# One transformer layer on sixteen images: the order of all five engines taken from written lists

## The chip, the cores and the metric

The kernel runs on one core of a Trainium2 chip. The metric is the device time of one execution in microseconds; lower is better. A core has five instruction streams that run side by side and meet only at semaphores: PE (TensorE, matrix products), ACT (ScalarE, table functions such as sine and exponential), DVE (VectorE), POOL (GpSimd) and SP (SyncE, which here only issues DMA transfers). Each stream is executed strictly in the order in which the program was written, so an instruction that waits holds up everything behind it on its engine.

## What is computed

Sixteen images are cut into patches, 1024 tokens of 256 numbers each; then comes one attention layer with a special treatment of the keys, and one mixture-of-experts network. Cut to what matters here:

```python
h = patches @ W.T + b                        # 1024 tokens x 256, per image
n = layernorm(h)
q, k, v = split(n @ w_qkv)                   # 8 heads of 32
k = sum(a[f]*sin(f*k) + b[f]*cos(f*k) for f in 1..256)
attn = softmax(q @ k.T * 32**-0.5)           # 1024 x 1024 per head
h = h + (attn @ v) @ w_out + b_out
n = layernorm(h)
shared = mlp3(n)                             # 256 -> 256 -> 128 -> 256
gated = two best of four experts, weighted   # 256 -> 128 -> 64 -> 256 each
h = h + shared + gated
```

## The kernel before

The sum over 256 frequencies is not taken term by term. The angles of one key channel are written to DRAM, read back and copied over the partitions (`load_waves`, the DMA `w<-ud`), multiplied by whole numbers on POOL (`turn_waves`, L1009) and put through a sine on ACT (`sine`, L1019). PE mixes two such tiles with the coefficients into a tile `kan` of PSUM (`mix`, L1039), DVE multiplies that by a third sine tile (`times_fast`, L1053, the tile named `f`), and PE adds up the products (`add_up`, L1072). This is one group of 8 key channels; an image has 32 groups, and after every eighth the finished keys of two heads are split in a high and a low part on DVE (`finish_keys`, L617 and L618), written to DRAM (`kd`), and read back stacked (`stack_keys`, `k<-kd`).

Attention runs in rounds. A round treats two heads and 512 queries, and has eight score tiles, one for each 128 keys; an image has eight rounds. For a score tile PE makes two matmuls of 512 columns (`score`, L1137, the tile `sT`). ACT takes the exponential (`exponential`, L1154): for an even tile into SBUF (`es`), for an odd one in place in PSUM. DVE then adds the odd tile to the even one before it (`pair_sum`, L1169, the tile `both`): these are the sums of two tiles of keys, by which the denominators are added up for two key tiles at once. PE weighs the values (`weigh`, L1184: `es` with the values, `both` with the values and with ones), and DVE normalizes at the end of the round (L1208, L1213, L1225).

Two resources tie this together. The PSUM pool `big` has two buffers of 1024 columns, and both the `kan` tiles of `mix` and the score tiles take them in turn. A score tile can therefore begin only when the reader of the tile two places before it is done: the exponential for an even score tile, the pair sum for an odd one, the product L1053 for a `kan` tile. And the wave tiles have eight buffers (`NW`), so a load waits for the mix of four groups earlier.

The rest (tokens, norms, keys, queries, values, gates, networks, projection) runs as four chains of small steps, numbered 0 to 3, which use two smaller PSUM buffers. A step of a chain that may take either form (`ANY`) is made as whole 128 x 128 matmuls or as four matmuls of 32 columns side by side, whichever fits its neighbours on PE (`tiling_of`). PE works in three tilings: whole, 128 x 32 (weighing, adding up, split steps) and 64 x 32 (mixing).

All instructions are written in an order which a planner in the kernel finds before it is built. PE's order is written out by hand in `ORDER`: M is a mix, R an adding up, S a score tile, W a weighing, a digit a step of that chain; one stretch of 240 letters covers an image and is repeated eleven times. The other four engines have no list: `others` goes through SP, POOL, ACT and DVE and takes, up to PE's clock, the step that would be ready first by the planner's own clocks, with a cost for each step given by hand (`put(ACT, "fixed", 0.99, ...)`). On ACT the sines, the loading of the exponential's table (`table`) and the exponentials of a round stand in one queue, `fixed`, in the order in which they were put there; only chain steps come between them.

Of the kernel before, what the change touches and what calls it, by code (L numbers as in the profile page):

```python
# [12 lines left out]
AF = mybir.ActivationFunctionType  # L13
# [44 lines left out]
LAG, LANDS, TABLE, PER_COLUMN = 0.06, 2.0, 1.28, 1.0 / 600  # L58
SWITCH = {None: 0.21, (128, 32): 0.13, (64, 32): 0.13}

TILINGS = {"mix": (64, 32), "av": (128, 32), "red": (128, 32)}
USERS = {"M": "prod", "S": "exp"}
KINDS = {"M": "mix", "R": "red", "S": "score", "W": "av"}
COLUMNS = (128, 32)
ORDER = (
    "333333313133100003300M00M00R00MM0MR3M33",
    "RM3M33MR03MR303MMSS0WSSWRWSSS3S03WWMMWW",
    "RMWMSSSRSSSWWSSWWW3WMM0RM0WWSSSSSSSWWWSMWWWRM0WMMWMRSSSSWWSSSRWSWWWWMMWMRMSSWSSSSWSSWRW0"
    "MWMMWMWWSSSRSSWWSWRSWSWWWW0M00M0SSSWRMWSWS3SW3SMSWRW3WMWM3MRMSS1SSWSSWRSSWW3W3MMWWWMR1SS"
    "S0SSWWS3S1MSWR1WM30MWWWSWM1R01SM1WS1WWSS1RSS1S0W1W1WWWMM0RMSSS1SSW1SWSW1SMW1RWMWW01MMWM1"  # L70
    "SS1RSRSWWS1SS0S1W1MMWMMWRSWWWS1S1S0SS1WWS1S3RWW1WMW1M1WMMWSS1SRSS1RS1SWWW1SW31WWMMW3WM0S"
    "SR0S1S0SWWSS1SMW3RM1W0WMMW1RWMWSS1S3SS1SSWWRS31WWWWWWM103MS1SSW1WSRS3MSWWSSMW1WWRWM13MM1"
    "S3SSRMSWWS3WSS3R1SW0WWM1WM1W1RM0SS1SW1SSWSSWWSMW1W1RM0M1WW1MS1S1MRWS1SWRSWS0SS1WM1WMWWWS"
    "S0RM3S1WMS1SWWSS0SWRW3WW10MMW31MS1SS1WRSSW1MS1SSWWWRW1WW01",
    (
        "MM0R1MM1S1SS1SSWW1S0S1SRWW0WWWWMM1MMRS3SS1SS1SSWWRSWWWWW3W13MM0RMM3SSS1SSWRWWS1SSWW3WMW3"
        "WM311MRSM1SWSSS1WR3SS31SWW0WW1WM1MW1MM0SS1SRW1SWS0S1WSSWRWWWWM01MM10RM0SS1SW1SSWW1SSWRS1"
        "WWWWMM1MS0SSWRWMSW1S1SS3SWWRW3WW1MM31MMRS1SS1WWSS1SS1SWWRWWWW101"
    )
    * 11,  # L80
    "MM10RMS3SS1SS01SSWWWSM1RWWWW1WMM01MS1MR",
    "WSS1SS3WWSS3WRSWW1WW30MM1RMS1SS3SS1SWWSSWMW3RMM311WMWMWWSRSSR3S1SSWWWS13S0WW1WWMMW1M01MS"
    "1S1SSRRSW1SW1SSWW101WMWWMWMMRSSS1SSW1WS1RWSSWWW1MM1WMSWSSR0SSWW1MS1SW1W1S10RW1MMWWW0MRMS"
    "1SS1SS1SSWW1SWR0WW1W1WMMMW1SRSS1SSWW1MSWSWS1WR1MMWWWRMS1S0SWMS1SSWSRSW0WWWWW10M1M1SS0RSS"
    "MWWSSS1SMWWR1MWW1MW1WR1MMS1SWS1SWSWSS1SRWWW1WWMMR1M1MSS1SW1SS1SWSSWRWW1M1WW1MMMWSSSRSSWS"
    "SRWWS1WWWMMRWW1MM1SS1W1S1SWSSS1SRWW1WWMWM1WM1MRS1RSWS1SWSS1SSWWWW1WW1SS1WS1SS1SSWWWSSWWW"
    "W1SS1S1SWSWSSWWWWWW11110110111110101001000000101001000100",
)

@with_exitstack  # L90
def plain_path(ctx: ExitStack, tc: tile.TileContext, a: dict, out: bass.AP, verdict: bass.AP):
# [179 lines left out]
    def retile(tiling):  # L271

        same = now["tiling"] == tiling
        now["tiling"] = tiling
        return 0.0 if same else SWITCH[tiling]

# [53 lines left out]
    def step(c):  # L330
# [9 lines left out]
        if on:  # L340
            at = max(clock[on], ch["ready"] + LAG)
            if on == PE:
                at = max(at, banks(c)[0][0] + LAG)
            ch["ready"] = clock[on] = at + (need[1] or 0.0)
            if bank is not None:
                free[bank] = ch["ready"]
        elif isinstance(need, tuple):
            ch["ready"] = max(ch["ready"], done[need])
# [11 lines left out]
        if on == PE:  # L360
            took = PER_COLUMN * (now["stream"] - before) + retile(now["piece"])
            now["piece"] = None
            ch["ready"] = clock[PE] = at + took
# [16 lines left out]
    def wanting(engine):  # L380

        for c, ch in enumerate(chains):
            need = ch["need"]
            if ch["gen"] is None or callable(need) or need[0] != engine:
                continue
            if engine == ACT and len(need) > 2 and now["table"] != need[2]:
                continue
            at = max(clock[engine], ch["ready"] + LAG)
            if engine == PE:
                if not banks(c):  # L390
                    continue
                at = max(at, banks(c)[0][0] + LAG)
            yield at, c

    def lay(engine, queue):
        cost, deps, key, action = queues[engine][queue].pop(0)
        at = begin(engine, deps)
        clock[engine] = at + cost
        done[key] = clock[engine]
        action()  # L400

    def heads(engine):
        for rank, (name, steps) in enumerate(queues[engine].items()):
            at = begin(engine, steps[0][1]) if steps else None
            if at is not None:
                yield at, rank, name

    def others(limit):

        soonest = None  # L410
        again = True
        while again:
            again = False
            soonest = None
            for engine in (SP, POOL, ACT, DVE):
                while True:
                    settle()
                    best = min(heads(engine), default=None)
                    chain = min(wanting(engine), default=None)
                    if chain and (  # L420
                        best is None
                        or chain[0] < best[0]
                        or (chain[0] == best[0] and best[2] not in ("sum", "prod", "keys"))
                    ):
                        at, lay_it = chain[0], lambda c=chain[1]: step(c)
                    elif best:
                        at, lay_it = best[0], lambda q=best[2]: lay(engine, q)
                    else:
                        break
                    if at > limit:  # L430
                        soonest = at if soonest is None else min(at, soonest)
                        break
                    lay_it()
                    again = True
        return soonest

    def lay_fixed(kind):

        cost, deps, key, action = queues[PE][kind][0]
        user = USERS.get(kind)  # L440
        if kind == "S" and key[2] % 2:
            user = "sum"
        at = begin(PE, deps + (bigs[-2:-1] if user else []))

        def lay_it():
            queues[PE][kind].pop(0)
            clock[PE] = done[key] = at + cost + retile(TILINGS.get(KINDS[kind]))
            if user:
                bigs.append((user, *key[1:]))
            action()  # L450

        return at, lay_it

    def run():

        order = "".join(ORDER)
        for i, token in enumerate(order):
            now["ahead"] = order[i + 1 : i + 4]
            while True:
                soonest = others(clock[PE])  # L460
                if token in KINDS:
                    at, lay_it = lay_fixed(token)
                else:
                    c = int(token)
                    at = next((at for at, one in wanting(PE) if one == c), None)
                    lay_it = lambda: step(c)
                if at is not None and (soonest is None or at <= max(soonest, clock[PE])):
                    break
                assert soonest is not None
                others(soonest)  # L470
            lay_it()
        while (soonest := others(clock[PE])) is not None:
            others(soonest)
        assert not any(q for e in queues.values() for q in e.values())
        assert not any(ch["gen"] for ch in chains)
# [4 lines left out]
    def load_x(b, j):  # L480

        b, j = b + j // (N // XT), j % (N // XT)
        if b < B:
# [5 lines left out]
            done["x", b, j] = transfer(1.75, 0.6, clock[PE])  # L489
# [38 lines left out]
    def tokens(b, half):  # L528
# [5 lines left out]
        for t in range(4):  # L534
# [14 lines left out]
            yield DVE, 0.41  # L549
# [95 lines left out]
    def values(b):  # L645
# [5 lines left out]
        for t0 in range(0, NT, 2):  # L651
# [12 lines left out]
            yield ACT, 0.5  # L664
# [7 lines left out]
            yield DVE, 0.6  # L672
# [134 lines left out]
    def networks(b, half, late=False):  # L807
# [25 lines left out]
        def first_of_expert(e):  # L833
            yield ANY
            ps = hidden(lambda c: w1e[:, 2 * e + c, :], "e1p")
            yield ACT, 0.6
# [4 lines left out]
        def second_of_experts(u, e1):  # L841
# [11 lines left out]
            yield ACT, 0.6  # L853
# [15 lines left out]
        for m in range(2):  # L869
            yield ANY  # L870
            ps = hidden(lambda c, m=m: w1s[:, c, ts(m, P)], "s1p")
            yield ACT, 0.6
# [14 lines left out]
        yield ACT, 0.6  # L887
# [57 lines left out]
    def load_waves(g, j):  # L945
# [13 lines left out]
        put(SP, "waves", 1.1, deps, ("load", g, j), action)  # L959
# [29 lines left out]
    def spread_waves(g):  # L989
# [11 lines left out]
        put(DVE, "spread", 1.28, deps, ("spread", g), action)  # L1001

    def turn_waves(g, j):
# [8 lines left out]
        put(POOL, "turn", 1.87, [dep], ("turn", g, j), action)  # L1012

    def sine(g, j, change):
        def action():
            now["table"] = AF.Sin
# [6 lines left out]
        put(ACT, "fixed", 0.96 + change, [("turn", g, j)], ("sine", g, j), action)  # L1023
# [26 lines left out]
    def times_fast(g):  # L1050
# [4 lines left out]
        put(DVE, "prod", 1.16, [("mix", g), ("sine", g, 2)], ("prod", g), action)  # L1055
# [76 lines left out]
    def score(att, kc):  # L1132
# [13 lines left out]
        put(PE, "S", 0.47, deps, ("score", att, kc), action)  # L1146

    def exponential(att, kc):
        def action():
            now["table"] = AF.Exp  # L1150
# [6 lines left out]
        put(ACT, "fixed", 0.99, deps, ("exp", att, kc), action)  # L1157
# [8 lines left out]
    def pair_sum(att, kc):  # L1166
# [5 lines left out]
        put(DVE, "sum", 1.16, deps, ("sum", att, kc), action)  # L1172
# [28 lines left out]
    def normalize(att):  # L1201
# [8 lines left out]
        def divide(half):  # L1210
# [11 lines left out]
            put(DVE, "norm", 0.4, deps, ("divide", att, half), action)  # L1222
# [15 lines left out]
        put(DVE, "norm", 1.67, [("av", att, NT - 1)], ("reciprocal", att), reciprocal)  # L1238
# [819 lines left out]
```

## Time and profile before

| | us |
|---|---|
| time, median of 4 runs (lowest to highest) | 3971.72 (3963.89 to 3976.18) |
| the profiled execution's own time | 3968.66 |
| its span in the profile | 3967.1 |

| engine | busy us | share of the span |
|---|---|---|
| PE, matmuls | 3728.9 | 94% |
| ACT | 3259.5 | 82% |
| POOL | 3192.2 | 80% |
| DVE | 3115.3 | 79% |
| the 16 DMA engines, hardware queue of SP | | 79.2% |

From the first mix of one image to the first mix of the next it takes, in the repeated part, 236 to 239 us. A matmul's end in the profile is modelled, and matmuls overlap; the time at which PE begins one is the surer number. "PEld" is the loading of a matmul's weights, which runs beside the matmul before it.

### The profile page before, as it was taken

What the parts mean: (1) busy time and instruction counts of PE and PEld (TensorE: products, weight loads), DVE (VectorE), ACT (ScalarE), POOL (GpSimd) and SP (SyncE); (2) the same over time, 40 slices, a digit from 0 to 9 for tenths busy, and PEclk for the clock granted to TensorE, in tenths of its full rate; (3) what the DMA queues carried; (4) which work ended last, traced back from release to release, by engine and by line L of the source; (5) the groups of instructions that cost most, each with busy time, mean ns of one, the idle gap of its engine ahead of it and who ended that gap; (6) DMA issues with size and microseconds to landing.
All of it is one profiled execution on the core that took longest, in us unless ns stands there. A gap on an engine that the chain in (4) does not pass through costs nothing. (4 is left out here: it accounts for less than half of the span.)

```text
span 3967.1 us, 93620 instructions
## 1 busy us (share of the span) xinstructions
PE 3728.9 (94%) x35701; PEld 1810.2 (46%) x35701; DVE 3115.3 (79%) x4715; ACT 3259.5 (82%) x3875; POOL 3192.2 (80%) x2312
## 2 busy tenths in 40 slices
PE   7888999999999999999999999999999999999988
PEld 4324344454544545444454544545454454534434
DVE  4667878888787887878878787888878888787873
ACT  2687888888888888898888888888888888888983
POOL 4878888788887888878888888878878888888860
PEclk9899999999999999999999999999999999999999
DMA  7877878888888788878879788788889888788750
GB/s 234 263 226 214 254 216 243 249 228 254 225 245 245 220 255 233 251 218 246 251 229 261 219 252 247 220 250 242 245 224 248 246 234 255 216 234 242 220 160 21
DMA packets 587580, 915.93 MB, mean 231 GB/s; under 512 B 58828, under 2 KB 177524, under 8 KB 587124
## 3 DMA queue, kind: packets, MB, share of 16 engines
q1 hardware_dynamic: 580880, 906.98, 79.2%
q8 instruction: 285, 4.67, 0.5%
q10 hardware_dynamic: 6244, 2.88, 0.3%
q14 instruction: 171, 1.40, 0.1%
HBM read 758.64 MB, written 150.99 MB: 229 GB/s over the span
## 5 line engine op out<-in xcount | busy, mean ns | idle before, releaser
L1009 POOL TENSOR_TENSOR w<-w,lane 128x1024 int32<-128x1024 int32 x1024 | 1925.2, 1895 | 387.8 <-DMA w<-ud 250.1
L1019 ACT ACTIVATE w<-w 128x1024 f32<-128x1024 int32 x1024 | 1011.5, 1047 | 51.5 <-POOL w L1009 47.2
L1009 POOL TENSOR_TENSOR f<-f,lane 128x1024 int32<-128x1024 int32 x512 | 970.4, 1895 | 102.8 <-DVE f L994 99.4
L1137 PE MATMUL sT<-q,k 128*128 128x512 f32 x2048 | 749.4, 465 | 160.3 <-DVE both L1169 53.9
L1169 DVE TENSOR_TENSOR both<-sT,es 128x1024 f32<-128x1024 f32 x512 | 624.9, 1220 | 309.5 <-ACT sT L1154 302.8
L1154 ACT ACTIVATE sT<-sT 128x1024 f32<-128x1024 f32 x512 | 517.5, 1011 | 264.3 <-PE sT L1137 195.5
L1053 DVE TENSOR_TENSOR f<-kan,f 128x1024 f32<-128x1024 f32 x512 | 609.3, 1215 | 146.1 <-ACT f L1019 93.6
L994 DVE STREAM_SHUFFLE f<-src 128x1024 int32<-128x1024 int32 x512 | 688.6, 1363 | 0.4
L1154 ACT ACTIVATE es<-sT 128x1024 f32<-128x1024 f32 x512 | 521.5, 1019 | 126.7 <-PE sT L1137 117.3
L1137 PEld LDWEIGHTS sT<-q,k 128*128 128x128 f32 x2048 | 346.1, 193 | 556.5 <-ACT es L1154 171.2
L1039 PE MATMUL kan<-w,coef 64*32 64x512 f32 x8192 | 557.2, 603 | 21.7 <-ACT w L1019 20.2
L1019 ACT ACTIVATE f<-f 128x1024 f32<-128x1024 int32 x512 | 517.3, 1047 | 0.0
L1184 PE MATMUL av<-both,v 128*32 128x256 f32 x4096 | 326.0, 389 | 3.3 <-DVE both L1169 3.1
L1184 PE MATMUL av<-es,v 128*32 128x256 f32 x4096 | 323.6, 387 | 3.4 <-DVE rc L1225 3.2
L1184 PE MATMUL av<-both,ones 128*32 128x256 f32 x4096 | 321.2, 384 | 0.0
L1072 PE MATMUL red<-f,pack 128*32 128x512 f32 x2048 | 300.5, 613 | 4.1 <-DVE f L1053 2.3
L1208 DVE RECIPROCAL rc<-av 128x256 f32<-128x256 f32 x128 | 224.6, 1755 | 66.7 <-PE av L1184 66.5
L1039 PEld LDWEIGHTS kan<-w,coef 64*32 64x32 f32 x8192 | 119.4, 105 | 304.4 <-issue 126.1
L301 PE MATMUL tok<-wt,x 128*128 128x256 f32 x960 | 227.0, 388 | 15.7 <-DMA x<-in_xT 12.5
L301 PEld LDWEIGHTS tok<-wt,x 128*128 128x128 f32 x960 | 181.6, 193 | 72.8 <-issue 20.4
L1184 PEld LDWEIGHTS av<-es,v 128*32 128x32 f32 x4096 | 110.6, 109 | 195.1 <-issue 153.2
L1184 PEld LDWEIGHTS av<-both,v 128*32 128x32 f32 x4096 | 115.0, 110 | 169.1 <-issue 95.5
(154 smaller groups left out, 4823.4 us busy)
## 6 DMA issues: line engine op xcount, KB each, us to landing
w<-ud SPq DMA_DIRECT2D x2048, 256.0 KB
q<-qd SPq DMA_DIRECT2D x512, 128.0 KB
k<-kd SPq DMA_DIRECT2D x128, 512.0 KB
x<-in_xT SPq DMA_DIRECT2D x128, 384.0 KB
ud<-u SPq DMA_DIRECT2D x64, 512.0 KB
ud<-ui SPq DMA_DIRECT2D x64, 512.0 KB
src<-ud SPq DMA_DIRECT2D x512, 64.0 KB
qd<-qhi SPq DMA_DIRECT2D x64, 256.0 KB
```

What stands on the lines that cost most here:

```text
L301: nc.tensor.matmul(out=out, lhsT=lhsT, rhs=rhs, start=start, stop=stop)
L994: nc.vector.stream_shuffle(w, sources[g // 8].rearrange("p r n -> p (r n)"), [4 * (g % 8) + i // 8 for i in range(32)],)
L1009: nc.gpsimd.tensor_tensor(w, w, f.to_broadcast([P, N]), ALU.mult)
L1019: nc.scalar.activation(x, w, AF.Sin, scale=TURN * 2.0**-32)
L1039: nc.tensor.matmul(out=ps[ds(64 * j + 32 * blk, 32), ts(r, 512)], lhsT=coef[ts(r, 64)].rearrange("p e f j -> p (e f j)"), rhs=w[ts(r, 64), ...
L1053: nc.vector.tensor_mul(w, kan.pop(g), w)
L1072: nc.tensor.matmul(out=rows_of_pair[p][ts(2 * i + r, 32), :], lhsT=pack[:, ds(PACK0 - 16 * (k % 2) - 2 * (k // 2), 32)], rhs=prod[:, ts(r, ...
L1137: nc.tensor.matmul(out=ps[:, ts(s, 512)], lhsT=k4[:, 2 * s + kc // 4, ts(kc % 4, P)], rhs=q4[:, s, :], start=True, stop=True,)
L1154: nc.scalar.activation(es, ps, AF.Exp, scale=SCALE)
L1169: nc.vector.tensor_add(both, scores[kc], exps[kc - 1])
L1184: nc.tensor.matmul(out=acc[0][ts(i, HD), ts(half, 256)], lhsT=ones32 if half else v[:, kc, p % NPAIR, ts(i % 2, HD)], rhs=es[:, ds(512 * ( ...
L1208: nc.vector.reciprocal(rc[0], acc[0][:, 256:512])
```

## The change

The kernel computes the same things with the same instructions. What is changed is the planner:

- `ORDER` becomes `ORDERS`, with a list for each of the five engines. A letter stands for the next step of one of the engine's queues (`TOKENS`), a digit for a chain's step.
- `others`, `wanting`, `heads` and the choice by readiness are taken out. `run` now takes, of the five lists' heads, the one that begins first, writes it, and goes on; the planner's clocks only decide how the five lists are interleaved in the program, and which of the two small PSUM buffers, and which tiling of an `ANY` step, is taken.
- On ACT the queue `fixed` is split in `sine`, `exp` and `table`, so a list may put sines between the exponentials of a round, or load the table at another place.
- The planner's constants and costs are changed (lag, landing of a transfer, table, switch of tiling, a stall, tails, and the steps' costs).
- The repeated stretch is given nine times instead of eleven; the images before and after it have lists of their own.

```diff
-LAG, LANDS, TABLE, PER_COLUMN = 0.06, 2.0, 1.28, 1.0 / 600
-SWITCH = {None: 0.21, (128, 32): 0.13, (64, 32): 0.13}
+LAG, LANDS, TABLE, PER_COLUMN, STALL = 0.07, 2.3, 1.29, 1.0 / 600, 0.15
+TAIL = {"pe": 0.27, "act": 0.08, "dve": 0.06, "pool": 0.0, "sp": 0.0}
+SWITCH = {None: 0.15, (128, 32): 0.12, (64, 32): 0.12}
...
+TOKENS = {
+    ACT: {"s": "sine", "e": "exp", "t": "table"},
+    DVE: {"u": "sum", "p": "prod", "k": "keys", "n": "norm", "d": "spread"},
+    POOL: {"o": "turn"},
+    SP: {"c": "source", "w": "waves", "k": "keys", "q": "queries"},
+}
...
-ORDER = (
...
-        "MM0R1MM1S1SS1SSWW1S0S1SRWW0WWWWMM1MMRS3SS1SS1SSWWRSWWWWW3W13MM0RMM3SSS1SSWRWWS1SSWW3WMW3"
-        "WM311MRSM1SWSSS1WR3SS31SWW0WW1WM1MW1MM0SS1SRW1SWS0S1WSSWRWWWWM01MM10RM0SS1SW1SSWW1SSWRS1"
-        "WWWWMM1MS0SSWRWMSW1S1SS3SWWRW3WW1MM31MMRS1SS1WWSS1SS1SWWRWWWW101"
-    )
-    * 11,
...
+ORDERS = {
+    PE: (
...
+            "MM10MM1RSS1S1SSW1WS1S0SWR0WWWWWMM1MMRS3SS1SSWWWSSWRS3W1WWW3M1M0RMM3SS1SRSS1WSSWW"
+            "WSWW3WMW3M31MSR1MS1SWR1SWSW3SS31SW0W1WMWWM10MMR1SS1SRSS10SSWW1WSWW1WW01MMW1RMM0S"
+            "S1S0SSWWW1SSRWS1WWWWMM1MS0SSWRMSW1SR1SS3SWWW31WWWMM13MM1SSRRS1SWS1SSW1SWWWWWW101"
+        )
+        * 9,
...
+    ACT: (
...
+            "ssss1s0s1ssss1sst1eee01e1eee0esssssssss0sssteeeee33e33ee3sssss3ssssssssteeeeeeee"
+            "sssss1s1s1s1ss1se1e133ee323e3e3e12tessss1sssss1ssst1ee1eee1ee1ess1ssssssssss1tee"
+            "ee1eeeesssssssssssseee111t1e1ee1eesssss1ssssssst2ee1e1ee12ee1e"
...
+    def head(engine):
+
+        if not orders[engine]:
+            return None
+        token = orders[engine][0]
+        if token.isdigit():
+            at = wanted(engine, int(token))
+            return at is not None and (at, lambda: step(int(token)))
+        queue = token if engine == PE else TOKENS[engine][token]
+        cost, deps, key, action = queues[engine][queue][0]
+        if engine == PE:
+            at = begin(PE, deps + (bigs[-2:-1] if user_of(token, key) else []))
+            return at is not None and (at, lambda: lay_fixed(token, at))
         at = begin(engine, deps)
...
+        return at is not None and (at, lambda: lay(engine, queue, at))
...
+        settle()
+        while any(orders.values()):
+            ready = {e: h for e in orders if (h := head(e))}
+            engine = min(ready, key=lambda e: ready[e][0])
+            token = orders[engine].pop(0)
+            now["ahead"] = orders[PE][:3]
+            ready[engine][1]()
+            settle()
...
-        put(ACT, "fixed", 0.96 + change, [("turn", g, j)], ("sine", g, j), action)
+        put(ACT, "sine", 0.946, [("turn", g, j)], ("sine", g, j), action)
...
-        put(ACT, "fixed", 0.99, deps, ("exp", att, kc), action)
+        put(ACT, "exp", 0.91, deps, ("exp", att, kc), action)
...
-        put(ACT, "fixed", TABLE + 0.2, [], ("table", rd), table)
+        put(ACT, "table", 0.11, [], ("table", rd), table)
```

## The prediction

> **What bounds the kernel now.** I read the page's totals first, then its groups of instructions, then who waited for whom, then stretches of one image each, and last a timeline of one pause.
>
> ```profile
> span 3967.1 us, 93620 instructions
> PE 3728.9 (94%) x35701; PEld 1810.2 (46%) x35701; DVE 3115.3 (79%) x4715; ACT 3259.5 (82%) x3875; POOL 3192.2 (80%) x2312
> ...
> L1137 PE MATMUL sT<-q,k 128*128 128x512 f32 x2048 | 749.4, 465 | 160.3 <-DVE both L1169 53.9
> L1169 DVE TENSOR_TENSOR both<-sT,es 128x1024 f32<-128x1024 f32 x512 | 624.9, 1220 | 309.5 <-ACT sT L1154 302.8
> L1154 ACT ACTIVATE sT<-sT 128x1024 f32<-128x1024 f32 x512 | 517.5, 1011 | 264.3 <-PE sT L1137 195.5
> L1039 PE MATMUL kan<-w,coef 64*32 64x512 f32 x8192 | 557.2, 603 | 21.7 <-ACT w L1019 20.2
> ```
>
> PE is busy 94%, the others about 80%. Of PE's 238 us of idle time (3967.1 - 3728.9), 160.3 stand before score matmuls; mixes have 21.7. The repeated images, from first mix to first mix:
>
> ```profile
> 1034.40:1272.90 238.50, 228.84 (x2227) 113.93 (x2226) 193.24 (x294) 203.39 (x244) 198.61 (x144) 0.99 0.83 239
> 1272.90:1510.10 237.20, 228.11 (x2235) 113.08 (x2238) 194.94 (x297) 203.37 (x243) 200.29 (x144) 0.99 0.84 242
> ```
>
> Columns: length, then busy time of PE, PEld, DVE, ACT, POOL, granted clock, DMA share, GB/s. Eleven such images average 237.6 us. One pause, in time order:
>
> ```profile
> 1372.07 0.74 PE L1137 MATMUL sT<-q,k 128*128 128x512 f32 x2
> 1372.74 0.64 PE L1184 MATMUL av<-es,v 128*32 128x256 f32 x8
> 1373.31 0.73 PE L1137 MATMUL sT<-q,k 128*128 128x512 f32 x2
> 1374.88 0.60 ACT L515 ACTIVATE hn<-h,less,rstd 128x256 f32<-128x256 f32 x1 [2.51 <-POOL less L507]
> 1375.38 1.00 ACT L1154 ACTIVATE sT<-sT 128x1024 f32<-128x1024 f32 x1
> 1376.42 1.23 DVE L1169 TENSOR_TENSOR both<-sT,es 128x1024 f32<-128x1024 f32 x1 [2.42 <-ACT sT L1154]
> 1377.70 2.08 PE L1137 MATMUL sT<-q,k 128*128 128x512 f32 x4 [3.66 <-DVE both L1169]
> ```
>
> Three score tiles in a row fill both buffers; ACT sits in a norm that waits for POOL, the exponential behind it is late, so is the sum, and PE stands 3.66 us.
>
> **PE's own work.** From matmul starts, 256 columns of float32 take 0.427 us, a score matmul 0.213. Counting the columns of all matmuls in both programs' orders gives 3313 us with 0.03 between the two halves of a score tile: the same before and after. A change of tiling costs 0.119 on average (starts of neighbours without a wait; 0.096 to 0.139), and the first score matmul after one 0.12 more: above, the tile at 1372.07 takes 0.67 until the next start, 0.43 + 0.12 + 0.12.
> - Before: 1485 changes x 0.119 = 176.7, 290 scores after one x 0.12 = 34.8: 3313 + 211.5 = 3524.5. A repeated image: 219.1 (86 changes).
> - After: 1695 changes = 200.8, 399 x 0.12 = 47.9: 3561.7. A repeated image: 221.4 (99 changes). This part loses 37.2 us, certainly.
>
> **The distance between score tiles.** What the new PE list buys is distance. A tile may start when the reader of the tile two before it is done. From the rows: 0.22 from the last column to the exponential's start, 1.01 for it, 0.03 to the sum, 1.22 for that, 0.05 back to PE: an even tile needs 1.28 us, an odd one 2.53, and more where ACT or DVE have something else in their lists between (taken at its own row's duration) or the exponential before is still running. The distance is PE's own work between, from its list. Summing only what is missing, in a repeated image:
> - before: 23 of its score tiles' successors come too early, 14.2 us. The worst are 0.46 (twice), 0.81, 0.92 and 1.23 us behind, as in `SWSSS1W`: there the third S starts 0.46 after the first has ended, one score tile (0.43 + 0.03); the first, an even tile, needs at least 1.28, so 0.82 is missing.
> - after: 14, 4.9 us; no three S stand in a row, and the worst distances are 0.81, 1.58, 1.66.
>
> Does such a count measure anything? Before, it makes 219.1 + 14.2 = 233.3, and 4.3 is left to 237.6; from PE's starts, the delay above the prices at score tiles alone is 13.9 per image. It does. Over the program (first three images / eleven / the rest) before: 94.5 + 155.7 + 39.8 = 290.0; after: 69.8 + 70.3 + 48.1 = 188.2. The gain is 101.8.
>
> **The other lists.** ACT, DVE and POOL run the same 3618, 4075 and 2311 instructions, SP the same 3745 transfers. ACT loads tables 309 times, not 257: 52 x 1.283 us = 67 us, all in the first four and last three images, none in the repeated ones (16 either way). An image has 237.6 - 203.4 = 34 us of free ACT time, and at most 12 more loads = 15.4 us, so they are hidden; those between exponentials are in the count. Without that cover the whole 67 would be lost. [...]
>
> DVE has 7.3 us of other work between a round's sums, not 5.1; that is in the count too. For SP and POOL the order decides which load stands behind which wait:
>
> ```profile
> 3468.38 7.62 DMA k<-kd
> ...
> 3566.24 6.14 DMA w<-ud
> ...
> 3752.41 4.46 DMA k<-kd
> ...
> 3887.83 0.93 PE sT L1137 x4
> ```
>
> These are pieces of the chain of work that ended last: start, length, what.
>
> In a repeated image the tightest key stack stands 10.0 us (before 11.9) of PE work ahead of its score, behind a wave load that waits for a mix; it needs 1.2 for that load's issue (an SP row, two transfers) and 4.46 to 7.62 from its own issue to landing, 5.7 to 8.8. The tightest wave load, now behind a query stack, stands 12.9 ahead of its mix (before 19.6) and needs 1.8 (issue of the queries), 6.1 to land, 1.9 on POOL and 1.0 for the sine, 10.8. Both fit, with 1 to 2 us to spare, and queued behind them are only loads with over 20. Bounds: nothing, or 2 us per image, 32; I take 0.5 per image, 8.
>
> **The sum.** 3967.1 = 3524.5 + 290.0 + 152.6; the rest is the start (about 70 us before the first mix), the tail, and 4.3 per image. I keep it. After: 3561.7 + 188.2 + 152.6 + 8 = 3910.5; 1.6 us lie around the span, and the median of the runs shown is 3.1 above the profiled run's 3968.66: **3915 us**.
>
> Beside this: after the pause of 3.66 us four score matmuls took 2.08, where four in the chain at 3887.83 take 0.93, so a long pause costs some 1.1 us extra. PE pauses over 3 us 13 times; without them 14 us less, my own range's lower side. [...]
>
> **Rivals.**
> - *The gain is larger.* If nothing queued on ACT and DVE held a reader up, the count after would be 78.7, not 188.2: 3915 - 109.5 = 3805. For it: orders of the readers were chosen too. Against it: before, the count with queues matched. Chance 0.08.
> - *The gain goes elsewhere: no change, 3970.* Scores wait no longer for buffers but for an engine. At 230.6 per image ACT would be at 88%, POOL at 86%; near that, a late instruction can't be made good. It needs 4 us per image. Against: mixes hardly wait now. Chance 0.10.
> - *Slower: SP's list.* If every key stack comes 1.5 us later than its score beyond the margin (four per image), that is 6 us x 16 = 96: 3907 + 96 = 4003. From 4 us per image on it decides (64.6 / 16). For it: the margins shrank to 10.0 and 12.9, and waits on a transfer are a fixed order's weak point. Against: scores waited for key stacks 11 times in the whole trace, 20.7 us. Chance 0.10.
> - The forecast: 0.72, its own range 3870 to 3955.
>
> The lists do take effect: PE's instructions stand in the new order. A measurement of this kernel can tell 0.3% (12 us) from no change. Faster: 0.69 + 0.08 + 0.03 = 0.80; same: 0.03 + 0.05 = 0.08; slower: 0.02 + 0.10 = 0.12. The range for 8 in 10 goes from 3855, halfway to the first rival, to 3966, near the second.
>
> **What would show it.** Idle before score matmuls well under 160.3, the sums' wait for the odd exponential under 302.8; repeated images near 230 to 232; 309 table loads; PE's streaming unchanged. It would be wrong if mixes or scores begin to wait for DMA, or if the repeated image stays at 237.

## The result, and the profile after

The kernel after takes 3966.40 us (median of 50 runs, 3939.82 to 3981.96), the kernel before 3971.64 us (median of 76 runs taken beside them, 3956.22 to 3983.62). The ratio is 0.9986, with a 95% interval from 0.9979 to 0.9992: 5 us of gain, where 57 were forecast. The profiled execution of after spans 3968.7 us, that of before 3967.1, so the two traces show two kernels that take the same time.

The page of the kernel after, totals and groups of instructions:

```profile
span 3968.7 us, 95230 instructions
...
PE 3717.3 (94%) x36493; PEld 1785.8 (45%) x36493; DVE 3124.0 (79%) x4715; ACT 3320.0 (84%) x3927; POOL 3191.9 (80%) x2312
...
L1254 PE MATMUL sT<-q,k 128*128 128x512 f32 x2048 | 739.9, 461 | 141.5 <-ACT es L1270 57.0
L1285 DVE TENSOR_TENSOR both<-sT,es 128x1024 f32<-128x1024 f32 x512 | 625.4, 1222 | 308.5 <-ACT sT L1270 300.4
...
L1189 PE MATMUL red<-f,pack 128*32 128x512 f32 x2048 | 288.8, 604 | 16.3 <-DVE f L1170 15.8
```

(Lines have moved: the score matmul L1137 is now L1254, the exponential L1154 is L1270, the sum L1169 is L1285, the mix L1039 is L1156.) Idle time before the score matmuls fell from 160.3 to 141.5 us, by 19 and not by 100. The sums still wait 300.4 us for the odd exponential (302.8 before). A wait that was small has grown: the packing matmuls of the product stood 4.1 us before and stand 16.3 now. Their line in the page of before:

```profile
L1072 PE MATMUL red<-f,pack 128*32 128x512 f32 x2048 | 300.5, 613 | 4.1 <-DVE f L1053 2.3
```

The instructions are not quite the same ones: ACT runs 52 more (3927 against 3875), all of them table loads, and PE runs 36493 matmuls instead of 35701, because some steps now take the other tiling.

Two repeated images of after, from first mix to first mix, in the stretches view (length; busy time of PE, PEld, DVE, ACT, POOL; granted clock, DMA share, GB/s):

```profile
1031.00:1272.70 241.70, 231.25 (x2299) 112.55 (x2298) 195.45 (x296) 203.59 (x246) 199.53 (x144) 0.98 0.84 238
1272.70:1511.90 239.20, 226.82 (x2302) 111.66 (x2302) 194.34 (x295) 202.93 (x244) 199.26 (x144) 0.99 0.83 236
```

They are no shorter than the two of before (238.50 and 237.20). Single images of the repeated part differ by more than was said above, in before from 235.2 to 240.8 us. Over images 4 to 10 (counted from 0, here and below) the mean is 238.3 us, in before 237.8; 230 to 232 were forecast.

**Where the delays stand.** From the start times of PE's records I took each score tile's delay beyond the columns and beyond the price of a change of tiling (0.116, and 0.12 more for a score behind one). That delay has two parts. The first is distance: what is missing until the reader of the tile two before would be done if nothing else held that reader up. The shortest gaps of waiting tiles give the need, start to start: 1.84 us behind an even tile, 3.09 behind an odd one, 2.55 behind a mix. The second part is all the rest: a reader that itself came late, a load that had not landed.

| whole program, us | before | after | difference |
|---|---|---|---|
| score tiles, distance | 65.7 | 22.1 | -43.6 |
| score tiles, rest of the delay | 136.2 | 138.1 | +1.9 |
| changes of tiling, and scores behind one, counted at that price | 207.1 | 244.5 | +37.4 |
| all else | 3549.4 | 3555.8 | +6.4 |
| start of the last matmul | 3958.4 | 3960.5 | +2.1 |

So the new list of PE did take two thirds of the short distances away. That was 44 us and not 102, and the changes of tiling that it adds come to 37 at their price. The larger part of the delays, 136 us, was not touched. The sizes depend on what a start without a wait is taken to cost: priced by the fastest third of the starts of each kind, distance is 82 us before and 28 after, 54 less, and the rest grows by 5. The picture is the same.

**What the untouched part is.** Three pauses recur in nearly every repeated image of after; the three timelines below are of after. Columns: start, length, engine, line, operation, and in brackets the idle time before it with what ended it.

```profile
1132.66 3.87 POOL L1127 TENSOR_TENSOR w<-w,lane 128x1024 int32<-128x1024 int32 x2 [4.14 <-DMA w<-ud]
...
1135.36 0.74 PE L1254 MATMUL sT<-q,k 128*128 128x512 f32 x2
...
1138.34 0.20 POOL L625 TENSOR_TENSOR less<-less,rstd 128x4 f32<-128x4 f32 x1
...
1138.58 1.09 ACT L633 ACTIVATE hn<-h,less,rstd 128x256 f32<-128x256 f32 x2 [2.46 <-POOL less L625]
1139.57 1.00 ACT L1270 ACTIVATE es<-sT 128x1024 f32<-128x1024 f32 x1
...
1140.63 0.73 PE L1254 MATMUL sT<-q,k 128*128 128x512 f32 x2 [2.84 <-ACT es L1270]
```

POOL waits 4.14 us for a load of waves; the norm's small steps stand behind two turns; ACT's list has the norm (L633) at its head and waits 2.46 us, and the exponential behind it, whose input is long there, holds PE up. This is score 11 of the image (of 64, counted from 0). It costs 3.4 us an image, in before 2.8.

```profile
1094.54 2.39 POOL L680 TENSOR_TENSOR h<-h,bout 128x1024 f32<-128x1024 f32 x1
...
1095.01 1.95 DVE L1351 TENSOR_SCALAR health<-health 128x8 f32<-128x8 f32 x1
...
1097.08 1.23 DVE L1170 TENSOR_TENSOR f<-kan,f 128x1024 f32<-128x1024 f32 x1
...
1098.36 1.05 PE L1189 MATMUL red<-f,pack 128*32 128x512 f32 x4 [0.66 <-DVE f L1170]
```

The image's check of its sums compares 128x8 numbers and takes 1.95 us, until POOL's addition beside it is done; the product stands behind it, and PE's packing step behind the product. This one is new, 1.75 us an image.

```profile
1210.35 1.21 SPq L1218 DMA_DIRECT2D k<-kd  x2
1212.26 7.64 SPq L1072 DMA_DIRECT2D w<-ud  x8
...
1219.51 0.70 PE L1254 MATMUL sT<-q,k 128*128 128x512 f32 x2 [2.25 <-DMA k<-kd]
```

A stack of keys is issued at 1210.35, with eight loads of waves behind it, and PE's score 32 waits for it until 1219.51. It costs 2.0 us an image, in before 1.6.

### The profile page after: what moved, and what is told of

Same layout as the page of the kernel before. It is cut to its first block, busy times and chain, and to the rows that moved or that the text cites. A ratio compares the mean times of both kernels' runs of the same rounds, so it can differ in the third digit from the quotient of the medians.

```text
span 3968.7 us, 95230 instructions
## 1 busy us (share of the span) xinstructions
PE 3717.3 (94%) x36493; PEld 1785.8 (45%) x36493; DVE 3124.0 (79%) x4715; ACT 3320.0 (84%) x3927; POOL 3191.9 (80%) x2312
## 5 line engine op out<-in xcount | busy, mean ns | idle before, releaser
L1254 PE MATMUL sT<-q,k 128*128 128x512 f32 x2048 | 739.9, 461 | 141.5 <-ACT es L1270 57.0
L1285 DVE TENSOR_TENSOR both<-sT,es 128x1024 f32<-128x1024 f32 x512 | 625.4, 1222 | 308.5 <-ACT sT L1270 300.4
L1270 ACT ACTIVATE sT<-sT 128x1024 f32<-128x1024 f32 x512 | 518.0, 1012 | 238.5 <-PE sT L1254 178.1
L1270 ACT ACTIVATE es<-sT 128x1024 f32<-128x1024 f32 x512 | 523.1, 1022 | 112.3 <-PE sT L1254 89.3
L1254 PEld LDWEIGHTS sT<-q,k 128*128 128x128 f32 x2048 | 345.4, 192 | 546.4 <-ACT es L1270 158.5
L1156 PE MATMUL kan<-w,coef 64*32 64x512 f32 x8192 | 558.2, 605 | 28.3 <-ACT w L1136 13.5
L1189 PE MATMUL red<-f,pack 128*32 128x512 f32 x2048 | 288.8, 604 | 16.3 <-DVE f L1170 15.8
L1156 PEld LDWEIGHTS kan<-w,coef 64*32 64x32 f32 x8192 | 119.5, 105 | 300.2 <-issue 113.6
L445 PE MATMUL tok<-wt,x 128*128 128x256 f32 x1008 | 235.7, 385 | 12.6 <-DMA x<-in_xT 10.6
L445 PEld LDWEIGHTS tok<-wt,x 128*128 128x128 f32 x1008 | 190.9, 192 | 60.8 <-issue 20.2
```

The lines of the kernel that those rows point to most:

```text
L445: nc.tensor.matmul(out=out, lhsT=lhsT, rhs=rhs, start=start, stop=stop)
L1156: nc.tensor.matmul(out=ps[ds(64 * j + 32 * blk, 32), ts(r, 512)], lhsT=coef[ts(r, 64)].rearrange("p e f j -> p (e f j)"), rhs=w[ts(r, 64), ...
L1189: nc.tensor.matmul(out=rows_of_pair[p][ts(2 * i + r, 32), :], lhsT=pack[:, ds(PACK0 - 16 * (k % 2) - 2 * (k // 2), 32)], rhs=prod[:, ts(r, ...
L1254: nc.tensor.matmul(out=ps[:, ts(s, 512)], lhsT=k4[:, 2 * s + kc // 4, ts(kc % 4, P)], rhs=q4[:, s, :], start=True, stop=True,)
L1270: nc.scalar.activation(es, ps, AF.Exp, scale=SCALE)
L1285: nc.vector.tensor_add(both, scores[kc], exps[kc - 1])
```

## The experiments

All times are ratios to the kernel before on the same chip, with the 95% interval; a difference of two such ratios is uncertain by about 0.0024, 10 us.

**The check without its comparison.** The edit:

```
-   nc.vector.tensor_scalar(sums, sums, SUM_MAX, None, ALU.is_le)
-   nc.vector.tensor_reduce(good[:, b : b + 1], sums, AX.X, ALU.min)
+   nc.vector.tensor_reduce(good[:, b : b + 1], sums, AX.X, ALU.add)
    ...
+   nc.vector.tensor_scalar(good, good, SUM_MAX, None, ALU.is_le)   # once, at the end
```

> The kernel after, with the image's check of its sums made of one reduction that adds the eight sums, instead of a comparison of the eight and a reduction; the comparison is made once at the end for all images (the bound is then put on the sum of an image's eight sums). In the trace of after the comparison of 128x8 takes 0.17 us in five images and 1.2 to 2.4 us in eleven, where a POOL addition of h and bout runs at the same time, and the product behind it on VectorE is what TensorE's packing step waits for, 1.75 us in each repeated image. Theory 1 (TensorE's own order paces the program, and a pause taken away is time won): 1.7 us in 9 to 11 images, 15 to 19 us less than after. Theory 2 (the period of an image, 238 us in both kernels, is set elsewhere, by the transfers or by POOL, and TensorE's pauses only take up the rest): no change, within 4 us of after.

Measured: 0.9952 (0.9935 to 0.9969), 13 us less than after, where 15 to 19 were expected. The timeline of this kernel at the same place in the next image:

```profile
1322.41 2.41 POOL L698 TENSOR_TENSOR h<-h,bout 128x1024 f32<-128x1024 f32 x1
...
1322.88 0.16 DVE L1369 TENSOR_REDUCE health<-health 128x1 f32<-128x8 f32 x1
1323.08 1.23 DVE L1188 TENSOR_TENSOR f<-kan,f 128x1024 f32<-128x1024 f32 x1
```

The reduction takes 0.16 us in all sixteen images, in ten of them beside this addition on POOL. In after the comparison takes 1.95 to 2.44 us in the eight images where this addition holds it up, 1.18 to 1.78 in three where POOL turns waves beside it, and 0.17 in the other five. It waits for no semaphore of POOL's, so one stream is held up by another here without one; by what, and why the reduction is not, no run shows. The pause was time, as theory 1 has it.

**Two exponentials ahead of the norm.** In ACT's list of the nine repeats:

```
-  se1e133ee323e
+  se1e1ee33323e
```

(s is a sine, e an exponential, a digit the next step of that chain; the 3s are the norm.)

> The kernel after, with one edit of ScalarE's list in the nine repeats: two exponentials stand ahead of the two steps of the norm that now wait about 2.5 us at the head of the list for POOL. In the trace of after TensorE's score 11 of each image stands 3 to 5 us, the last part of it for these exponentials. Theory 1 (pauses of TensorE are time): 2 to 2.5 us in each of nine images, 18 to 22 us less than after. Theory 2 (the period of 238 us is set elsewhere): no change, within 4 us of after.

Measured: 0.9939 (0.9921 to 0.9958), 19 us less than after. Who waited for whom in images 4 to 10 (total, times, longest), first in after, then here:

```profile
ACT hn L633 <- POOL less L625: 28.1, 14, 4.3
PE sT L1254 <- ACT es L1270: 26.5, 15, 4.6
...
PE sT L1254 <- DVE both L1285: 8.3, 8, 1.9
```

```profile
PE sT L1272 <- DVE both L1303: 18.1, 19, 1.9
...
PE sT L1272 <- ACT es L1288: 7.3, 12, 1.3
ACT hn L651 <- POOL less L643: 7.1, 8, 1.8
```

The wait for the exponential falls by 19 us, but 10 of them come back as waits for a sum: score 15 now stands about 2 us in each of these images. A pause is time, and part of it goes to the next in line.

**Lists put together from both kernels.** Both lists hold the same steps, so they can be cut wherever both have issued the same ones.

> All five engines run lists put together from those of after and of before, cut only where both have issued the same steps on every engine: after's for the first 1.5 images, before's up to 3.88, after's up to 13.81, before's up to 14.09, after's up to 15.88, before's for the rest. By the two traces after is 23.5 us ahead at 1.5 images, 4.0 at 3.88, 10.2 at 13.81, 2.5 at 14.09, 5.2 at 15.88 and behind by 2 at the end. Theory 1 (each stretch keeps its own time whatever stands before it): 19.5 + 7.7 + 7.3 = 34 us less than after, 36 less than before. Theory 2 (what one stretch gains another must give back, since the transfers or POOL set the pace): within 8 us of after.

Measured: 0.9954 (0.9938 to 0.9970), 13 us less than after, a little over a third of what theory 1 expected. By the starts of the mixes, this kernel leads before by 18.6 us at 1.5 images (424.5 against 443.1), where after leads by 23.5; at image 4 it leads by 7.0 (1027.4 against 1034.4). Before's own list for the stretch between thus did not keep its own time: a lead gained early is given back there. Theory 1 fails in the first four images. Besides, SP's stores and its loads of x are issued from inside the other engines' steps, and their places among the listed loads move with a splice. So the run does not show which engine takes the lead back.

**SP's list of before.**

> The kernel after with the list of SyncE's loads taken from before (430 of its 1472 places differ), the other four lists as in after. The rival of the prediction, that the new order of loads made waves and key stacks late, has the gain come back here: 10 us or more less than after. Theory 1 (the margins of the loads are the same in both, the pauses stand elsewhere): within 6 us of after.

Measured: 1.0246 (1.0230 to 1.0261), 103 us more than after. Neither expectation had a loss. Here scores wait 48.0 us for stacks of keys; in before and in after it is much less (total, times, longest):

```profile
PE sT L1137 <- DMA k<-kd: 20.7, 11, 3.4
```

```profile
PE sT L1254 <- DMA k<-kd: 24.2, 13, 3.3
```

So late stacks did not eat the gain: these waits grew by 3.5 us only from before to after, and taking the old list back makes them longer, not shorter. The rest of the scores' delays is 194.5 us here, against 138.1. But the loss is not in the repeated images: images 4 to 10 take 238.7 us on the mean, against 238.3 in after, while the first four together take 61 us more. The run shows that the other four lists need the list of loads that was made with them at the start of the program; for the repeated images it shows no difference between the two lists.

**The three edits together.**

> The three edits that each won time, in one kernel: the lists put together from after and before (cut at 1.5, 3.88, 13.81, 14.09 and 15.88 images), the two exponentials ahead of the norm in the nine repeats, and the image's check made of one adding reduction. Alone they came to 0.9954, 0.9939 and 0.9952 of before, that is 13, 19 and 13 us below after. Theory 1 (each pause of TensorE is time of its own): the three add up, 45 to 50 us below after, a ratio to before near 0.987; it would beat both kernels. Theory 2 (another chain stands just behind and takes over once some pauses are gone): not below the best of them by more than 8 us, a ratio of 0.992 or more.

Measured: 0.9915 (0.9899 to 0.9931), 28 us less than after: better than each, but not their sum of 45. Neither theory's number; what stands in their way is seen in the timeline of this kernel at score 15:

```profile
1368.85 3.75 POOL L1145 TENSOR_TENSOR w<-w,lane 128x1024 int32<-128x1024 int32 x2
...
1369.13 1.65 DVE L840 TENSOR_TENSOR gp<-gp,gs 128x16 f32<-128x16 f32 x1
...
1370.90 2.04 DVE L845 TENSOR_TENSOR over<-gp 128x12 f32<-128x12 f32 x3
...
1372.86 1.21 DVE L1303 TENSOR_TENSOR both<-sT,es 128x1024 f32<-128x1024 f32 x1
...
1374.12 0.72 PE L1272 MATMUL sT<-q,k 128*128 128x512 f32 x2 [1.09 <-DVE both L1303]
```

Tiny operations of the gate, of 128x16 and of 128x12 and smaller, both inputs in SBUF, take 1.65 and 2.04 us (the second is all three comparisons together) while POOL turns waves, and the sum behind them is what PE waits for. It looks like the hold-up at the check (1.95 us for 128x8); an experiment below tries that.

**The lists of before with two of the edits.**

> The lists of before on all five engines, written out (no other order than before's own), with the two edits that do not belong to the change: the check as one adding reduction, and the exponentials ahead of the norm at the same place in each image. In before the check's comparison cost 0.86 us at most and TensorE did not wait behind it; the pause at the norm was 2.7 us an image, against 3.3 in after. Theory 1 (before had part of these pauses too, and the lists of after lost their gain to the rest): 15 to 25 us less than before, a ratio of 0.994 to 0.996, so that the lists of after with the same edits stay ahead by 10 to 25 us. Rival (the shorter distances of after are worth nothing, whatever else is mended): the lists of before with the edits are as fast as after with them, a ratio near 0.988.

Measured: 1.0058 (1.0036 to 1.0080), 23 us slower than before, where both expectations had it faster. This run is inconclusive. PE, ACT, DVE and POOL keep before's order (ACT but for the exponentials moved), but SP's stores and loads of x fell in other places than in before, which the expectation did not allow for. Inside it, score 11 fell to 1.3 us while score 15 rose to 2.2 and score 32 from 1.6 to 2.8.

**More changes of tiling.** The edit:

```
-   if kind == "whole":
+   if kind in ("whole", "either"):
        return None
```

> The kernel after, in which every step that may run in either tiling of TensorE runs in the whole array: the columns streamed are the same, the changes of tiling rise from 1696 to 1965 and the score tiles behind a change fall from 399 to 361. Theory 1 (the price of a change that the prediction took, 0.119 us, and 0.12 for a score behind one, is paid in full): 269 x 0.119 - 38 x 0.12 = 27 us more than after, a ratio to before of 1.0055. Rival (changes of tiling lie in the shadow of waits): within 6 us of after, 0.997 to 1.000.

Measured: 1.0003 (0.9993 to 1.0014), 7 us more than after, not 27 (the rival had at most 6). Counted at their price, its changes of tiling come to 31.2 us more (4.6 off for scores behind one), but the rest of the scores' delays is 121.3 us instead of 138.1. The reading that fits is that a change ahead of a wait only fills the wait. The prediction's "certainly" was then too strong, and its 37 us are an upper bound.

**One distance undone.** In PE's list of the nine repeats:

```
-  SSWW1WSWW1WW01
+  SSWSW1WWW1WW01
```

> The kernel after with one distance undone: in each of the nine repeats the 24th score tile is issued three steps earlier, behind one weighing matmul instead of two and a step of the networks. The changes of tiling stay 1696. Counted as the prediction counted, the tile would start 1.3 us before the sum of the tile two before it is done. Theory 1 (a short distance is paid in full, so the count of distances was right where nothing else stands in the way): 9 x 1.3 = 12 us more than after, a ratio to before of 1.0015. Rival (what one distance saves, the next wait takes, so that distances are worth nothing): within 4 us of after, 0.9976 to 0.9996.

Measured: 1.0025 (1.0013 to 1.0036), 15 us more than after, where theory 1 had 12. By the split above, the distance part is 31.3 us instead of 22.1, the rest unchanged (138.4). So this short distance is paid in full: nothing else stands in its way.

**The gate's comparisons with an input in PSUM.** On the three edits:

```
+   logits = small("gwt")
+   nc.vector.tensor_copy(logits, ps)
    ...
-   over[:, :, d, 0 : NE - d], p[:, :, 0 : NE - d], p[:, :, d:NE], ALU.is_ge
+   over[:, :, d, 0 : NE - d], ps[:, :, 0 : NE - d], logits[:, :, d:NE], ALU.is_ge
```

> The kernel with the three edits, and the gate's three comparisons of 128x12, 128x8 and 128x4 made on the logits in PSUM against a copy of them, a step earlier, instead of on the probabilities in SBUF (equal logits then decide as equal probabilities did). In the trace with the three edits these comparisons take 2.0 to 3.6 us together where POOL turns waves at the same time, against 0.16 us each where it doesn't, and the sum behind them on VectorE is what TensorE's score 15 of each image waits for, 0.4 to 2.0 us, 15 us in the program. Theory (VectorE's small operations stand still while POOL holds something that both need, when all their inputs lie in SBUF; with an input in PSUM they don't): the comparisons take under 0.7 us together, 10 to 15 us less than with the three edits, a ratio to before of 0.988 to 0.989. Rival (the wait moves to the next in line, the norm's copies or POOL): within 4 us of the three edits, 0.9905 to 0.9925.

Measured: 0.9899 (0.9883 to 0.9915). The two groups of the largest comparison, first with the three edits, then here (busy, mean ns):

```profile
L845 DVE TENSOR_TENSOR over<-gp 128x12 f32<-128x12 f32 x32 | 27.0, 845 | 0.0
```

```profile
L838 DVE TENSOR_TENSOR over<-gateT,gwt 128x12 f32<-128x12 f32 x32 | 5.4, 170 | 1.1
```

The comparison falls from a mean of 845 ns to 170. At score 15 the pause is gone: in images 4 to 10 its mean delay falls from 1.8 to 0.3 us. So the comparisons are no longer held up, as the theory expected: the three have means of 170, 156 and 154 ns (845, 291 and 336 with the three edits), while the gate's product of 128x16, both inputs in SBUF, still has 586 (730). That the input in PSUM does it, and not the earlier place, was not shown by itself. But the time falls by only 6 us against the three edits, which is less than two ratios can tell apart and lies between the theory and the rival; whether this pause was time is not shown.

**The stack of keys in two halves.** On the three edits:

```
-   for j in range(2):
-       nc.sync.dma_start(out=k4.bitcast(FP)[ts(j, 64), :, 0:512], in_=src)
+   for half in range(2):
+       for j in range(2):
+           nc.sync.dma_start(
+               out=k4.bitcast(FP)[ts(j, 64), half::2, 0:512], in_=src[:, half::2, :]
+           )
```

> The kernel with the three edits, and each stack of keys loaded by four transfers of half the size instead of two, those of the first four tiles of keys ahead of the others, so that the first scores wait for half the bytes. Score 32 to 34 of each image now wait 0.4 to 3.5 us for the stack, 34 us in the program. Theory (the pause is the landing of 1 MB at the DMA's share of 0.84): the first half lands about 2 us earlier, 15 to 20 us less than with the three edits, a ratio to before near 0.987. Rival (SyncE pays for 128 more issues, 0.55 us each, and the loads of waves that follow come later): no gain or a loss, 0.991 to 0.996.

Measured: 0.9850 (0.9830 to 0.9869), 26 us less than with the three edits, more than the 15 to 20 expected. There, PE's scores still waited

```profile
PE sT L1272 <- DMA k<-kd: 31.0, 15, 3.6
```

and here no score waits for the stack any more; the idle time before scores falls from 137.7 to 115.5 us, so 9 of the 31 us come back as other waits. In images 4 to 10 most of the wait for the stack comes back at the next scores: score 34 now stands 1.29 us behind the exponential in each of them. These seven images gain only 2 us together; most of the 26 us lies ahead of them and behind them. The additional issues on SP (256 transfers of 256 KB instead of 128 of 512 KB) cost nothing that can be seen.

**Both with the three.**

> Both of the last two edits with the three. Theory 1 (each pause is time of its own): the gains add up, 25 to 35 us less than with the three edits, a ratio to before of 0.983 to 0.985. Rival (another chain stands close behind, so that pauses taken away come back in part): 0.987 or more.

Measured: 0.9834 (0.9816 to 0.9853), 32 us less than with the three edits, a median of 3897.32 us: the fastest here, below both kernels. The gains add up as theory 1 had it.

**Three edits of code on both kernels.** These are the check as one reduction, the gate's comparisons and the stack of keys in halves, with the lists untouched: once on after, once on before.

> The kernel after with its own five lists untouched and three edits of code only: the image's check as one adding reduction, the gate's comparisons with an input in PSUM, the stack of keys in four transfers with the first tiles of keys ahead. By the runs so far these three came to 14, 10 and 28 us. Theory 1 (the pauses they take away stand in after and hid what the lists had won): 45 to 52 us less than after, a ratio to before of 0.985 to 0.987. Rival (they only pay together with the other lists): 0.990 or more.

> The kernel before, its own order untouched, with the same three edits of code. Theory 1 (the lists of after take 44 us of short distances away, pay 38 us at most for changes of tiling, and lose the rest at pauses that these edits mend in both): before gains only 20 to 30 us by the edits, a ratio of 0.993 to 0.995, so that the lists of after are then 25 us or more ahead, 0.6%. Rival (the lists of after are worth nothing in themselves): before with the edits is within 8 us of after with them, 0.985 to 0.988.

Measured: after 0.9851 (0.9834 to 0.9869), before 0.9938 (0.9921 to 0.9955). The page's lines, first before with the edits, then after with them:

```profile
span 3943.2 us, 93717 instructions
...
L1142 PE MATMUL sT<-q,k 128*128 128x512 f32 x2048 | 741.8, 461 | 152.7 <-ACT es L1159 62.0
```

```profile
span 3915.2 us, 95392 instructions
...
L1277 PE MATMUL sT<-q,k 128*128 128x512 f32 x2048 | 737.1, 459 | 119.0 <-ACT es L1293 75.5
```

The same edits are worth 25 us on before and 54 on after, and the lists of after, which were 5 us ahead, are now 35 ahead ((0.9938 - 0.9851) x 3972, give or take 10). The split of the scores' delays: distance 68.8 before and 21.9 after, about as without the edits; the rest 127.3 and 118.0. Both expectations named theory 1 hold, and both rivals are out: with these edits the lists of after have a gain of their own. Of the 29 us between 54 and 25, some 13 are the check (by the first experiment), a pause that PE has in after alone.

Where this gain stands can be read from the starts of the mixes, in one trace of each kernel (positive: after is the faster of the two, us):

| images | without the edits | with them |
|---|---|---|
| 0 and 1 | +18.0 | +18.1 |
| 2 to 4 | -17.2 | +3.6 |
| 5 to 13 | +9.7 | +13.4 |
| the rest (start, 14, 15 and end) | -12.6 | -8.0 |
| start of the last matmul | -2.1 | +27.1 |

The lead of the first two images is there in both columns. Without the edits it is lost in images 2 to 4, with them it is kept. In images 4 to 10, where the repeated lists run, the two kernels with the edits take 235.8 (before) and 235.2 us: there the shorter distances and the additional changes of tiling nearly cancel. So what the edits brought out is above all a lead at the start of the program, not a shorter repeated image.

## Why the prediction was wrong

**PE sets the time: right.** Taking the pause at the check, at the norm or at the stack of keys away in the lists of after shortened the program, and the one distance undone lengthened it. The lists of before with two such edits did not become faster, and that run stays unexplained; in the first four images the spliced lists do not add up either.

**PE's own work, 37.2 us lost: right as a price, wrong as a certainty.** The counts at the price in the traces give 37.4. (1695 x 0.119 is 201.7 and not 200.8, so the prediction's own sum is 38.1.) But 269 further changes, counted at 27, cost 7 us, which fits changes that lie in a wait.

**The distance between score tiles, 101.8 us gained: this is the step that failed.** The count had 290.0 us missing before and 188.2 after. The chip shows delays at scores of 201.9 and 160.2 us in all, of which 65.7 and 22.1 are distance; the gain in distance is 43.6. The count took two things for one. It let a reader be late by whatever stood ahead of it in ACT's or DVE's list, at that instruction's own duration, and took the result for something that distance mends. The traces have a rest of 136.2 us before and 138.1 after that the new distances leave as it is. Its sizes were off on both sides: the prediction's first rival puts 78.7 of the 188.2 to distance alone and so 109.5 to queues, where the trace has 22.1 and 138.1. How the 290.0 divides, the prediction does not say, and why its count of distance alone came out too high stays open.

The count was accepted because of one agreement, 14.2 us counted against 13.9 found in a repeated image of before. That agreement was luck. By the split, a repeated image of before has 3.1 us of distance (21.9 in seven images) and 7.9 of other delays (55.0), 11.0 in all; why the prediction's reading of the starts gave 13.9, it does not say. The largest of the other delays are a late norm at ACT's head (2.8) and a stack of keys that had not landed (1.6). The count has neither wait, since it takes each instruction at its own duration, and neither became shorter with the new distances (3.4 and 2.0 in after). A sum that meets the total proves little about its terms; the pauses had to be compared place by place, and the traced pause that the prediction itself shows (ACT in the norm, waiting for POOL) was the largest of those that distance does not govern.

**The other lists, 8 us lost to SP: small.** All else grew by 6.4 us. The new wait at the check (12 us, R behind the product) is in it. The 52 additional table loads are there (309 in the trace, as counted). Of them 32 stand in images 1 to 3, where after takes 239.2, 247.9 and 246.2 us against 243.1, 242.7 and 237.3. No run took the loads alone away. But with the three edits of code the same loads stand in the same images, which then take 233.2, 242.3 and 235.5 us, each less than in before with these edits (238.2, 244.7 and 236.0): so the loads alone do not make them slow. Image 4 of after, which has none of them, is slow too (241.7 against 238.5).

**The rivals.** What came is the second, no change, and its reason was the right one in part: scores wait for an engine and for a load instead of for buffers. It was priced as a shortage of ACT's and POOL's time at 86 to 88%. What the runs show is a matter of order: an instruction at the head of a list that waits, and others behind it that could run. The third, key stacks late through the new list of SP, is not what happened: scores wait 24.2 us for them instead of 20.7. The first, a larger gain, was off further than the forecast.

**The sum again.** 3958.4 - 43.6 + 1.9 + 37.4 + 6.4 = 3960.5. With the distance term at its measured size, the prediction's own steps would have given 3524.5 + 290.0 + 152.6 = 3967.1, less 43.6, plus 37.2, plus 8: 3968.7, no change. That this is the span measured, to the tenth, is luck too: the 8 us stood for loads, and what they meet are the check and other small terms.

## What to carry to other kernels

Before a gain is computed from a model of waits, list the recurring pauses of the trace by place and name what ends each; only those that the change governs may be in the sum, and an agreement of totals is no test of that. When a new order moves the time little, mend the recurring pauses in both versions, compare again, and look where in the program the difference stands: here the same three edits of code brought the two orders from 5 us apart to 35, and most of that lies in the first images and not in the repeated ones. In an order fixed beforehand, an instruction whose input comes late belongs behind those whose inputs are there (19 us here), and a load of which the first consumers need one half can be sent with that half ahead (26 us here).

## What the chip showed beyond that

Whether POOL's addition holds up the image's check on DVE is decided within a few hundredths of a microsecond. In images 5 to 12 of after the check's comparison starts 0.01 to 0.04 us ahead of POOL's addition; it takes 2.42 to 2.44 us in seven of them and 0.17 in one. In the spliced kernel, with the same lists in these images, it takes 0.17 us in six of the eight. In both traces together the comparison was held up in every case where it started 0.013 to 0.029 us ahead (nine), and never where it started 0.032 to 0.042 us ahead (seven). So in these sixteen cases a start 0.029 us ahead was not enough; the order of the instructions is fixed, the outcome is not.

Single runs of one and the same kernel differ by up to 1% (3939.82 to 3981.96 us in after), and with them the granted clock: over the runs of after for which both are known, from 0.980 to 0.988, a time longer by 3.3 us goes with each 0.001 of clock less (correlation -0.77). Inside one trace, that of before, the granted clock is 1.00 from 1374.0 to 1377.2 us, 0.50 from 1377.3 to 1380.6, where the score matmuls behind the pause of 3.66 us run, and 1.00 again from 1380.7 to 1384. Whether the pauses bring the lower clock about, or the other way round, was not tried.
